# Layer 0 attention from the third batch on: scores computed once with queries on partitions, the softmax weights turned by VectorE and transfers

## The chip, the core and the metric

The kernel runs on one NeuronCore of a Trainium2 chip. TensorE (PE) multiplies matrices into PSUM banks; VectorE (DVE) reduces, copies and transposes 32x32 blocks; ScalarE (ACT) evaluates exp and other functions; GpSimd (POOL) does a few elementwise jobs; SyncE (SP) issues nearly all transfers (DMA), one after the other. Every engine works off its own instructions in order and waits on semaphores of the others. The metric is the device time of one execution in microseconds (us).

## The reference, cut to what matters

Two layers run over x (8 batches, 256 tokens, 256 features) with a context of the same shape. Each layer adds a gated cross-attention and a gated feed-forward part to x. The change touches the attention of layer 0:

```
q = Q @ Wq + bq          # Q = layernorm(x), K = V = context
k = K @ Wk + bk          # 16 heads of 16 features
v = V @ Wv + bv
scores = einsum('bhqd,bhkd->bhqk', q, k) / sqrt(16)
attn = softmax(scores, axis=-1)
out = einsum('bhqk,bhkd->bhqd', attn, v)
return out @ Wo + bo
```

Layer 0's feed-forward part ("slots") follows for the same batch, then layer 1's attention (8 heads of 128, 512 keys: 256 of the context and 256 of x), then layer 1's quantized feed-forward part over all batches.

## The kernel before, in words

Layer 1's attention is the main loop: `attention1` goes through 64 steps, one for each batch and head. A step computes scores for the two halves of the queries (line 1170), their negative maxima (VectorE, line 1171), exp (ScalarE, line 1172) and the division by the sums (lines 1173, 1174); `move_e` turns the weights with two VectorE transposes of 32x32 blocks (line 1184) and four SP transfers (line 1190) from the tile z into eT, where keys lie on partitions; `sums` multiplies them with the values (line 1226) one step later. Projections for the next heads are lines 1087 (queries), 1124 (keys), 1147 (values) and 1239 (output).

Layer 0 is ahead of it. Batches 0 and 1 run in a head stage before the loop; batches 2 to 7 are cut into pieces with costs and put into a queue (`side`), together with the slots' pieces. Each step of the loop spends a share of that queue, so that batch b's layer 0 is finished when the loop needs it: `until` forces it at head 5 of the batch before. The order that comes out is fixed when the program is built.

In layer 0 heads go in groups of four (`HG`), four groups a batch. float32 numbers are split into a rounded part hi and a rest lo, so that one matmul with single-pass operands sums hi*hi, hi*lo, lo*hi and lo*lo over 64 rows. Before the change a group of a batch past the second does this:

- `stack`: six transfers fetch the operand rows of four heads from DRAM (lines 624 and 628), where `split` had written hi and lo (line 528).
- `scores`: eight matmuls of 65 rows (line 648) with queries on partitions, four maxima (line 651), and their split into hi and lo (lines 654, 655).
- `maxima`: a TensorE transpose (line 661) and two ScalarE copies (line 664) put the maxima into further operand rows.
- `exps`: eight matmuls of 73 rows (line 674), which compute the scores a second time with keys on partitions and the maxima subtracted, and four exp of 512 columns (line 677).
- `sums`: eight matmuls of 32 columns (line 685), in float32, which the profile counts as two each; `divide`: a transpose and two small operations on VectorE (lines 708 to 711).

float32 matmuls of layer 1 count twice in the profile as well: the eight instructions of line 1226 in one step are four matmuls in the code.

Of the kernel before, what the change touches and what calls it, by code (L numbers as in the profile page):

```python
# [25 lines left out]
HG = 4  # L26
NG = H0 // HG
NROW = 4 * DK0

# [20 lines left out]
IDLE_KEY = 10  # L50
IDLE_LATENTS = 8
# [55 lines left out]
def flamingo_kernel(ctx: ExitStack, tc: tile.TileContext, a: dict, out: bass.AP):  # L107
# [62 lines left out]
    wk_n, wq_n = xs[4], cs[4]  # L170
    wk, wq = (w0.tile([P, 2, D], F32, tag=n, name=n) for n in ("wk", "wq"))
    bk_n, bq_n = (pp_.tile([P, 2], F32, tag=n, name=n) for n in ("bkn", "bqn"))
    bk, bq = (w0.tile([P, 2], F32, tag=n, name=n) for n in ("bk", "bq"))
    nc.sync.dma_start(out=cs[0], in_=c_in[0])
    nc.sync.dma_start(out=wk_n, in_=a["L0_xattn_Wk"].rearrange("(c p) n -> p c n", p=P))
    nc.sync.dma_start(out=xs[0], in_=x_in[0])
    nc.sync.dma_start(out=wq_n, in_=a["L0_xattn_Wq"].rearrange("(c p) n -> p c n", p=P))
    for t, name in ((bk_n, "L0_xattn_bk"), (bq_n, "L0_xattn_bq")):
        nc.sync.dma_start(out=t, in_=a[name].rearrange("(c p) -> p c", p=P))
# [14 lines left out]
    def load_by_place():  # L194
        for m in range(2):
            for t, name in ((bk, "L0_xattn_bk"), (bq, "L0_xattn_bq")):
                bias = a[name].rearrange("(h e) -> e h", e=DK0)
                nc.sync.dma_start(out=t[:, m : m + 1], in_=bias[m * 8 : (m + 1) * 8, :])

    def by_place():  # L200
        for t, n in ((wk, wk_n), (wq, wq_n)):
            A.copy(t.rearrange("p c (e h) -> p c e h", e=DK0), n.rearrange("p c (h e) -> p c e h", e=DK0))
        G.tensor_scalar(bq4, bq, DK0**-0.5, None, ALU.mult)

# [4 lines left out]
    pick = w0.tile([NMAX, HG], F32, tag="pick", name="pick")  # L209
    V.tensor_tensor(pick, ident[:NMAX, 1 : 1 + HG], ident[:NMAX, 1 + HG : 1 + 2 * HG], ALU.add)  # L210

    def operand_pairs(pool, n):

        pairs = []
        for i in range(n):
            q = pool.tile([NROW + NMAX, HG, S], F32R, tag=f"qs{i}", name=f"qs{i}")
            k = pool.tile([NROW + NMAX, HG, S], F32R, tag=f"ks{i}", name=f"ks{i}")
            V.tensor_copy(q[NROW : NROW + 1, :, :], blank[:1, :HG, None].to_broadcast([1, HG, S]))
            V.tensor_copy(k[NROW:, :, :], pick[:, :, None].to_broadcast([NMAX, HG, S]))
            pairs.append((q, k))  # L220
        return pairs

    blank = w0.tile([P, 2 * HG], F32, tag="blank", name="blank")
    V.memset(blank, 0.0)

    pairs_a, pairs_b = operand_pairs(pp_, 2), operand_pairs(w0, 2)
# [104 lines left out]
    slotsT = pp_.tile([P, 2, P], F32, tag="slotsT", name="slotsT", bufs=1)  # L331
# [29 lines left out]
    def prepare_slots():  # L361
        st = {}

        def load_slots():
# [7 lines left out]
            st["w2"] = pp_.tile([NSLOT, P], F32, tag="w2n", name="w2n")  # L372
# [92 lines left out]
    bq4_n = pp_.tile([P, 2], F32, tag="bq4n", name="bq4n")  # L465
    G.tensor_scalar(bq4_n, bq_n, DK0**-0.5, None, ALU.mult)

    def values_tile(pool):
# [6 lines left out]
        s: [pool.tile([P, SIDE + NMAX], F32R, tag=f"nm{s}{i}", name=f"nm{s}{i}") for i in range(3)]  # L475
        for s, pool in (("a", pp_), ("b", w0))
# [7 lines left out]
    class Batch0:  # L484
# [11 lines left out]
        def tmp(self, dtype=F32, name="t"):  # L496
            if self.b == 0:
                return own[name]
            return self.pool.tile([P, 2, S], dtype, tag="t", name=name, bufs=4)

        def halves(self, name):
            if self.b > 1:
                return self.tmp(F32R, "hi"), self.tmp(F32R, "lo")
            return (
                pp_.tile([P, 2, S], F32R, tag=f"{i}{name}{self.b}", name=f"{i}{name}") for i in ("hi", "lo")
            )
# [10 lines left out]
        def split(self, name, full):  # L517

            hi, lo = self.halves(name)
            V.tensor_copy(hi, full)  # L520
            eng = V if self.b < 2 else G
            eng.tensor_tensor(lo, full, hi.bitcast(F32), ALU.subtract)
            if self.b < 2:
                return hi, lo
            name += self.s
            d = dram.tile([2, D, S], F32, tag=f"d{name}", name=f"d{name}")
            for i, x in enumerate((hi, lo)):
                nc.sync.dma_start(out=d[i].rearrange("(m p) t -> p m t", p=P), in_=x.bitcast(F32))
            return d.rearrange("i (e h) t -> i e h t", e=DK0)
# [9 lines left out]
        def turn_c(self):  # L539
            self.cT = self.pool.tile([P, 2, S], F32, tag="cT", name="cT", bufs=1)  # L540
            A.copy(self.cT, self.turned(cs[self.b]))
# [21 lines left out]
        def query(self):  # L563
            w, bias = (wq_n, bq4_n) if self.b < 2 else (wq, bq4)
            pp = self.project(w, self.xnT)
            q = self.tmp(name="q")
            for m in range(2):
                A.activation(q[:, m, :], pp[:, m, :], AF.Identity, bias=bias[:, m : m + 1], scale=DK0**-0.5)
            self.dq = self.split("q", q)

        def key(self):
            w, bias = (wk_n, bk_n) if self.b < 2 else (wk, bk)
            pp = self.project(w, self.cT)
            k = self.tmp(name="k")
            for m in range(2):
                A.activation(k[:, m, :], pp[:, m, :], AF.Identity, bias=bias[:, m : m + 1])
# [39 lines left out]
        def stack(self, g):  # L616

            if self.b < 2:
                return self.spread(g)
            q, k = self.pairs[g % 2]  # L620
            at = slice(g * HG, (g + 1) * HG)
            for i in range(2):
                half = 2 * DK0 * i
                nc.sync.dma_start(
                    out=k[half : half + 2 * DK0, :, :].bitcast(F32), in_=self.dk[:, :, at, :]
                )
            for r in range(4):
                ins = nc.sync.dma_start(
                    out=q[r * DK0 : (r + 1) * DK0, :, :].bitcast(F32), in_=self.dq[r // 2][:, at, :]
                )  # L630
# [48 lines left out]

        def sums(self, g):  # L680

            po = self.bank()[:, :S]

            def product(kc, j):
                return T.matmul(  # L685
                    po[32 * j : 32 * j + 32, :],
                    self.ve[:, kc, g * HG + j, :],
                    self.e[j // 2][:, j % 2, kc, :],
# [29 lines left out]
        def turn_o(self):  # L718

            self.oT = self.tmp(name="oT")  # L720
            V.transpose(
                self.oT.rearrange("p c (i s) -> p (c i) s", s=32), self.o.rearrange("p c (i s) -> p (c i) s", s=32)
            )
# [15 lines left out]
    def layer0():  # L739
# [8 lines left out]
        def head(me, groups):  # L748
# [6 lines left out]
            ] + [piece(0.0, me, "stack", g) for g in groups]  # L755

        def maxima(me, g):
            return [piece(0.5, me, "scores", g, qc) for qc in range(2)] + [piece(0.1, me, "maxima", g)]

        for b in range(2):  # L760
            out[b] += head(bs[b], range(2)) + maxima(bs[b], 0)
        for b in range(B):
            me = bs[b]
            after = bs[b + 1] if 0 < b < B - 1 else None
            for g in range(NG):
                nxt = (me, g + 1) if g + 1 < NG else (after, 0)
                far = (me, g + 2) if g + 2 < NG else (after, g + 2 - NG)
                work = [piece(0.5, me, "exps", g, 0)]
                if nxt[0]:
                    work.append(piece(0.5, nxt[0], "scores", nxt[1], 0))  # L770
                work.append(piece(0.5, me, "exps", g, 1))
                if nxt[0]:
                    work.append(piece(0.5, nxt[0], "scores", nxt[1], 1))
                if g == 0:
                    work.append(piece(1.8, me, "value"))
                if after:
                    if g == 0:
                        work.append(piece(0.0, after, "norm"))
                    if g == 1:
                        work.append(piece(0.5, after, "turn_x"))  # L780
                        work.append(piece(0.5, after, "turn_c"))
                        work.append(piece(1.8, after, "query"))
                    if g == 2:
                        work.append(piece(1.8, after, "key"))
                if nxt[0]:
                    work.append(piece(0.1, nxt[0], "maxima", nxt[1]))
                work.append(piece(1.8, me, "sums", g))
                if far[0]:
                    work.append(piece(0.0, far[0], "stack", far[1]))
                work.append(piece(0.0, me, "divide", g))  # L790
                out[b] += work
        for b in range(B):
            out[b] += [piece(0.0, bs[b], "turn_o"), piece(1.8, bs[b], "finish")]
# [194 lines left out]
    for b in range(2, B):  # L988
        side.add(merge(work0[b], waiting, 1, 2))
# [12 lines left out]
    load_by_place()  # L1002
# [12 lines left out]
    for n, go in enumerate(first):  # L1015
# [3 lines left out]
        if n >= LAG:  # L1019
            second.pop(0)()  # L1020
    by_place()
# [5 lines left out]
    prep_cm.__exit__(None, None, None)  # L1027

# [15 lines left out]
    class Batch1:  # L1044
# [5 lines left out]
        def media(self):  # L1050
# [5 lines left out]
            else:  # L1056
                self.cn = at1.tile([P, 2, D], F32, tag="tn", name="cn")
            ln_apply(self.cn, cs[self.b], *ln_stats(cs[self.b], "c"))

        def latents(self):  # L1060

            b = self.b
            self.ln = at1.tile([P, 2, D], F32, tag="tn", name="ln")
# [72 lines left out]
        def value(self, hp, half, early=False):  # L1136

            if hp not in self.v:
                v = at1.tile([P, 4, 2 * P], F32, tag="v1", name="v1")
                self.v[hp] = [v[:, 0:2, :], v[:, 2:4, :]]  # L1140
            if half == 0 and early:
                self.v[hp][0] = (own["oT"], own["o"])[hp]
# [11 lines left out]
            (A.copy if half == 0 else V.tensor_copy)(self.v[hp][half], pv)  # L1154
# [58 lines left out]
        def sums(self, h):  # L1213
# [11 lines left out]
            for kc in range(4):  # L1225
                T.matmul(  # L1226
                    pi,
                    self.v[h // 2][kc // 2][:, kc % 2, (h % 2) * P : (h % 2 + 1) * P],
# [26 lines left out]
        def norm(self):  # L1255
            b = self.b
            self.xl = at1.tile([P, 2, D], F32, tag="tn", name="xl") if b < B - 1 else ffn["xl"]
# [173 lines left out]
    def attention1():  # L1431
# [24 lines left out]
        for n, (b, h) in enumerate(steps):  # L1456
# [19 lines left out]
            elif last is not None:  # L1476
                if h == 1 and b > 0:
                    bs[b - 1].project(1)
                bs[last[0]].sums(last[1])
            if h == 2 and b > 0:  # L1480
# [15 lines left out]
            if h % 2 == 1 and nxt:  # L1496
                if nxt[0] > 0 or nxt[1] > 3:
                    bs[nxt[0]].value(nxt[1] // 2, 0)
                bs[nxt[0]].value(nxt[1] // 2, 1)
# [259 lines left out]
```

## Time and profile before

| what | us |
|---|---|
| device time, median of 3 runs (914.7 to 917.16) | 915.1 |
| the profiled execution, device time | 917.64 |
| its span in the trace | 915.7 |
| PE busy | 877.0 |
| DVE busy | 639.8 |
| ACT busy | 461.9 |
| POOL busy | 143.1 |

Busy time is the union of an engine's spans. The first loop step begins at 131.2 us (its first maximum), the 17th at 339.7, the 41st at 640.9; the last weights are used at 857. Layer 0's last pieces lie before 647 us, so the loop has a stretch that is dense with layer 0 (131.2 to 339.7), one with less of it (339.7 to 640.9) and one with none. After 857 layer 1's feed-forward part follows.

### The profile page before, as it was taken

The numbers are of one execution on the slowest core, as the hardware profiler recorded it, in microseconds if no ns is written. First come the engines' busy times: TensorE is split into PE (matmuls) and PEld (weight loads), VectorE is DVE, ScalarE is ACT, GpSimd is POOL, SyncE is SP. The second block draws the span as 40 slices with busy tenths as digits, with TensorE's granted clock in tenths as the row PEclk, the third lists the DMA queues.
The fourth block names the chain that finished last, engine by engine and source line by source line (L and its number), as shares of the span: only waits on it lengthen the run. The fifth ranks groups of instructions, "written<-read, shape, count | busy, mean of one in ns | idle before, by whom it ended". The sixth has DMA issues, their size and how long they took to land. (4 is left out here: it accounts for less than half of the span.)

```text
span 915.7 us, 12787 instructions
## 1 busy us (share of the span) xinstructions
PE 877.0 (96%) x4339; PEld 636.3 (69%) x4341; DVE 639.8 (70%) x1630; ACT 461.9 (50%) x915; POOL 143.1 (16%) x183
## 2 busy tenths in 40 slices
PE   5998999999999999999999999999989999999897
PEld 4766777887777767766777667666756776776645
DVE  9675788777587766767677665766895475455387
ACT  3676646555356542555544544554364335434394
POOL 7011130201110112111011000010510010000083
PEclk9999999999999999999999999999999999999999
DMA  6712303342341332332312322212323232222112
GB/s 165 250 10 69 114 29 90 88 120 77 108 116 47 92 92 47 84 98 73 92 37 68 104 69 71 46 47 64 107 64 70 47 69 59 58 55 60 24 35 92
DMA packets 71728, 71.12 MB, mean 78 GB/s; under 512 B 14640, under 2 KB 67184, under 8 KB 71664
## 3 DMA queue, kind: packets, MB, share of 16 engines
q1 hardware_dynamic: 70032, 69.53, 29.0%
q0 software_dynamic: 1632, 0.79, 0.5%
q8 instruction: 35, 0.57, 0.3%
q14 instruction: 29, 0.24, 0.1%
HBM read 28.08 MB, written 8.39 MB: 40 GB/s over the span
## 5 line engine op out<-in xcount | busy, mean ns | idle before, releaser
L1172 ACT ACTIVATE e<-bank_m,nm 128x512 f32<-128x512 f32 x128 | 88.0, 688 | 107.5 <-DVE nm L1171 105.3
L1171 DVE TENSOR_REDUCE nm<-bank_m 128x1 f32<-128x512 f32 x128 | 87.1, 686 | 60.1 <-PE bank_m L1170 59.1
L1226 PE MATMUL bank_m<-eT,v 128*128 128x256 f32 x496 | 121.5, 382 | 4.6 <-DMA eT<-z 4.3
L1226 PEld LDWEIGHTS bank_m<-eT,v 128*128 128x128 f32 x496 | 92.4, 190 | 35.7 <-issue 16.6
L1124 PE MATMUL bank_m<-kvT,w1kv 128*128 128x512 f32 (+1 forms) x256 | 115.9, 568 | 0.0
L1147 PE MATMUL bank_m<-w1kv,kvT 128*128 128x256 f32 x480 | 111.0, 380 | 0.0
L1170 PE MATMUL bank_m<-k,q 128*128 128x512 f32 x224 | 108.9, 598 | 0.0
L1147 PEld LDWEIGHTS bank_m<-w1kv,kvT 128*128 128x128 f32 x480 | 89.4, 190 | 12.0 <-issue 0.8
L1184 DVE STREAM_TRANSPOSE z<-e 128x512 f32<-128x512 f32 x126 | 88.6, 706 | 4.3 <-DMA eT<-z 1.8
L651 DVE TENSOR_REDUCE nf<-bank_z 128x2 f32<-128x512 f32 x112 | 74.0, 680 | 20.7 <-PE bank_z L648 20.6
L270 POOL TENSOR_TENSOR rstd<-rstd,mhalf 128x2 f32<-128x2 f32 x48 | 34.6, 722 | 298.0 <-DVE rstd L269 267.7
L677 ACT ACTIVATE e<-bank_z 128x512 f32<-128x512 f32 x112 | 63.5, 598 | 32.7 <-PE bank_z L674 31.8
L1124 PEld LDWEIGHTS bank_m<-kvT,w1kv 128*128 128x128 f32 x256 | 46.4, 190 | 43.1 <-issue 38.0
L1233 ACT ACTIVATE oT<-bank_m,bv 128x256 f32<-128x256 f32 x64 | 30.4, 474 | 81.1 <-PE bank_m L1226 81.0
L1087 PE MATMUL bank_m<-kvT,w1q 128*128 128x256 f32 x256 | 64.0, 385 | 1.3 <-DVE kvT L1077 0.9
L1174 DVE TENSOR_SCALAR e<-e,rs 128x512 f32<-128x512 f32 x128 | 63.3, 495 | 2.6
L1239 PE MATMUL bank_m<-w1o,oT 128*128 128x256 f32 x256 | 59.2, 380 | 0.6 <-DVE x L1253 0.6
L1170 PEld LDWEIGHTS bank_m<-k,q 128*128 128x128 f32 x224 | 41.0, 191 | 23.4 <-issue 17.0
L1087 PEld LDWEIGHTS bank_m<-kvT,w1q 128*128 128x128 f32 x256 | 48.1, 192 | 12.4 <-issue 3.9
L1239 PEld LDWEIGHTS bank_m<-w1o,oT 128*128 128x128 f32 x256 | 48.0, 190 | 10.2 <-issue 3.2
L674 PE MATMUL bank_z<-qs,ks 73*128 73x256 f32 x224 | 49.8, 325 | 3.2 <-DVE nf L651 2.6
L1154 DVE COPY v<-bank_m 128x512 f32<-128x512 f32 x32 | 22.0, 688 | 44.0 <-PE bank_m L1147 44.0
(386 smaller groups left out, 1482.0 us busy)
## 6 DMA issues: line engine op xcount, KB each, us to landing
eT<-z SPq DMA_DIRECT2D x252, 128.0 KB, 2.7
qs<-dqb SPq DMA_DIRECT2D x96, 64.0 KB, 2.5
ks<-dkb SPq DMA_DIRECT2D x48, 128.0 KB, 2.8
c<-in_ctx_dram SPq DMA_DIRECT2D x8, 256.0 KB, 2.9
x<-in_x_dram SPq DMA_DIRECT2D x8, 256.0 KB, 2.8
w1kv<-in_L_xattn_Wkv_dram SPq DMA_DIRECT2D x4, 512.0 KB, 6.8
out_dram<-y SPq DMA_DIRECT2D x7, 256.0 KB, 2.2
dqb<-hi SPq DMA_DIRECT2D x6, 256.0 KB, 3.0
```

The lines of the kernel that those rows point to most:

```text
L651: V.tensor_reduce(full[:, 2 * half : 2 * half + 2], ps, AX.X, ALU.max, negate=True)
L677: A.activation(e[:, i, :, :], ps, AF.Exp)
L1087: T.matmul(pq[:, i, :], w1q[:, c, h * P : (h + 1) * P], self.kvT[:, c, S:], start=c == 0, stop=c == 1,)
L1124: T.matmul(pk[:, at], w1kv[:, c, h * P : (h + 1) * P], self.kvT[:, c, at], start=c == 0, stop=c == 1,)
L1147: T.matmul(pv[:, k, :], (self.mT, self.kvT[:, :, S:])[half][:, c, k * P : (k + 1) * P], w1kv[:, c, at : at + 2 * P], start=c == 0, stop=c ...
L1170: T.matmul(ps, q, self.k[h], start=True, stop=True)
L1171: V.tensor_reduce(nm[:, at], ps, AX.X, ALU.max, negate=True)
L1172: A.activation(e[:, qc, :], ps, AF.Exp, bias=nm[:, at], accum_out=sums[:, at])
L1174: V.tensor_scalar(e[:, qc, :], e[:, qc, :], rs[:, at], None, ALU.mult)
L1184: V.transpose(z[:, :, :, qc, :].rearrange("p kq kc s -> p kc kq s"), self.e[h][:, qc, :].rearrange("p (kc kq k) -> p kc kq k", kc=4, kq=4),)
L1226: T.matmul(pi, self.v[h // 2][kc // 2][:, kc % 2, (h % 2) * P : (h % 2 + 1) * P], eT[:, kc], start=kc == 0, stop=kc == 3,)
L1239: self.projected = T.matmul(self.pp[:, qc, :], self.oT[:, h, qc * P : (qc + 1) * P], w1o[:, h, :], start=h == 0, stop=h == H1 - 1,).ins
```

## The change

For batches 2 to 7 the scores are computed once. `weigh` takes two heads (a pair s of a group): four matmuls, two maxima that ScalarE takes as the bias of exp, four exp of 256 columns, and, as layer 1 does, two VectorE transposes and four transfers that turn the weights. `scores`, `maxima` and `exps` remain for batches 0 and 1. The operand stacks hold one pair of heads and are two in number; `split` writes hi and lo interleaved, and a second copy with the two exchanged for q. `sums` reads the turned weights.

```diff
         def split(self, name, full):
...
-            name += self.s
-            d = dram.tile([2, D, S], F32, tag=f"d{name}", name=f"d{name}")
-            for i, x in enumerate((hi, lo)):
-                nc.sync.dma_start(out=d[i].rearrange("(m p) t -> p m t", p=P), in_=x.bitcast(F32))
-            return d.rearrange("i (e h) t -> i e h t", e=DK0)
+            d = dram.tile([2, 2 * D, S], F32, tag=f"d{name}", name=f"d{name}")
+            hl = hl.bitcast(F32)
+            nc.sync.dma_start(
+                out=d[0].rearrange("(m p i) t -> p m (i t)", m=2, i=2), in_=hl.rearrange("p m i t -> p m (i t)")
+            )
+            for i in range(2 if name == "q" else 0):
+                nc.sync.dma_start(
+                    out=d[1].rearrange("(m p i) t -> i p m t", m=2, i=2)[1 - i], in_=hl[:, :, i, :]
+                )
+            return d.rearrange("r (g s i n) t -> r g s n i t", s=2, i=2, n=HALF)
...
-        def stack(self, g):
...
+        def stack(self, g, s):
+
+            q, k = stacks[s]
+            for r in range(2):
+                at = slice(r * HALF, (r + 1) * HALF)
+                ins = nc.sync.dma_start(out=k[at, :, :].bitcast(F32), in_=self.dk[0, g, s])
+                ins = nc.sync.dma_start(out=q[at, :, :].bitcast(F32), in_=self.dq[r, g, s])
...
+        def weigh(self, g, s):
+            q, k = stacks[s]
+            e = at0.tile([P, 2, 2, S], F32, tag="e", name="e", bufs=2)
+            z = at0.tile([P, 8, 2, 2, 32], F32, tag="e", name="z", bufs=2)
+            for i in range(2):
+                ps = self.bank().rearrange("p (c k) -> p c k", c=2)
+                for qc in range(2):
+                    T.matmul(ps[:, qc, :], q[:, i, qc * P : (qc + 1) * P], k[:, i, :], start=True, stop=True)
+                nm = small.tile([P, 2], F32, tag="nm0", name="nm0")
+                V.tensor_reduce(nm, ps, AX.X, ALU.max, negate=True)
+                for qc in range(2):
+                    A.activation(e[:, i, qc, :], ps[:, qc, :], AF.Exp, bias=nm[:, qc : qc + 1])
+                V.transpose(
+                    z[:, :, i, :, :].rearrange("p kb c s -> p c kb s"),
+                    e[:, i].rearrange("p c (kb k) -> p c kb k", k=32),
+                )
+            eT = self.e[g, s] = at0b.tile([P, 4, 2, 2, 64], F32, tag="eT0", name="eT0", bufs=3)
+            for i in range(4):
+                nc.sync.dma_start(
+                    out=eT[:, i].rearrange("p kc h x -> p (kc h x)"),
+                    in_=z[32 * i : 32 * i + 32].rearrange("p kb h c s -> p (kb h c s)"),
+                )
```

The tags e and z share two buffers, so each has one. Further edits go with it:

- The pieces of a group are now: weigh pair 0 of the next group, stack pair 0 of the one after it, sums, weigh pair 1, stack pair 1, divide. The first group of batch 2 is stacked and weighed in the queue, no longer in the head stage. A batch's values and key projection and the finish of the batch before have new places in the list, and the slots' pieces come after every second piece and no longer after every one.
- The weights wk, wq and their biases are loaded straight into their tiles in the reference's order; the copies that permuted them (`by_place`) and four small loads (`load_by_place`) go.
- The key's ScalarE copy reads its columns in a permuted order, and the output's transposes (`turn_o`) are two of 256 columns instead of one of 512 (6 batches).
- To make room: the pool of batch temporaries (tag t) has two buffers for four, layer 1's `cn`, `ln` and `xl` share one buffer (tag tn) for two, and layer 1's values are kept by halves, three in number; the second half is computed in the step that uses it first instead of the step before:

```diff
+            if h % 2 == 0 and n > 0:
+                me.value(h // 2, 1)
...
-                bs[nxt[0]].value(nxt[1] // 2, 1)
```

## The prediction

> **What bounds the kernel now.** I read the busy rows first, then the busy time in five stretches cut at loop steps, then the costliest groups, then who waits for whom.
>
> ```profile
> PE 877.0 (96%) x4339; PEld 636.3 (69%) x4341; DVE 639.8 (70%) x1630; ACT 461.9 (50%) x915; POOL 143.1 (16%) x183
> ...
> PEclk9999999999999999999999999999999999999999
> ```
> ```profile
> core 0: us, PE busy (x) PEld busy (x) DVE busy (x) ACT busy (x) POOL busy (x), PEclk, DMA share, GB/s
> 0.00:131.20 131.20, 113.04 (x707) 88.02 (x708) 98.39 (x285) 76.31 (x137) 35.71 (x60) 0.97 0.39 111
> 131.20:339.70 208.50, 204.65 (x1088) 155.13 (x1087) 154.87 (x423) 112.52 (x225) 25.87 (x32) 0.99 0.33 89
> 339.70:640.90 301.20, 297.81 (x1441) 213.20 (x1441) 209.24 (x550) 145.44 (x293) 32.10 (x43) 1.00 0.27 70
> 640.90:857.00 216.10, 210.81 (x826) 149.30 (x825) 135.71 (x303) 93.47 (x209) 19.43 (x22) 0.99 0.27 65
> ```
>
> I call the stretches head, A (dense with layer 0), B (thinner) and C (no layer 0). In A and B PE idles 3.9 of 208.5 and 3.4 of 301.2 us; DVE idles 53.6 and 92.0. So PE sets both, and PE work taken out there shortens them until DVE, the next, is full. The groups give the prices:
>
> ```profile
> L651 DVE TENSOR_REDUCE nf<-bank_z 128x2 f32<-128x512 f32 x112 | 74.0, 680 | 20.7 <-PE bank_z L648 20.6
> ...
> L648 PE MATMUL bank_z<-ks,qs 65*128 65x256 f32 x224 | 50.0, 332 | 1.0 <-ACT e L677 0.5 <-ACT qs L614 0.3
> L674 PE MATMUL bank_z<-qs,ks 73*128 73x256 f32 x224 | 49.8, 325 | 3.2 <-DVE nf L651 2.6 <-ACT qs L664 0.6
> ...
> L654 DVE CAST nmb<-nf 128x4 fp32r<-128x4 f32 x56 | 9.5, 170 | 0.4
> ...
> L655 DVE TENSOR_TENSOR nmb<-nf,nmb 128x4 fp32r<-128x4 f32 x56 | 8.8, 156 | 0.5
> ...
> L661 PE MATMUL bank_z<-ident,nmb 128*73 128x128 f32 x28 | 7.9, 282 | 1.5 <-DVE nmb L655 1.5
> ```
> ```profile
> L1184 DVE STREAM_TRANSPOSE z<-e 128x512 f32<-128x512 f32 x126 | 88.6, 706 | 4.3 <-DMA eT<-z 1.8
> ...
> L1190 SPq DMA_DIRECT2D eT<-z x252: 542/598/1699, 135.5 to 848.5; - x126
> DMA to landing us min/median/max: 2.5/2.7/4.2
> ...
>   DMA eT<-z: 1.8, 3
> ```
>
> Matmuls overlap, so one costs its share of the busy time, 50.0/224 = 0.22 us, not its own 0.33. The last fence is the path that layer 0's weights will take: a transpose of 0.70, four issues of 0.60 on SP, 2.7 to land; and VectorE already waits for its z to be read, 1.8 us in three cases (last line, from the view of line 1184).
>
> **PE.** A group loses eight matmuls and a transpose; 24 groups: 192 x 0.22 + 24 x 0.28 = 42.2 + 6.7 = 49. By the instruction orders of the two built programs, cut at the same steps: single-pass score matmuls go from 152 to 136 in the head, 174 to 100 in A, 186 to 84 in B, line 661's transposes from 9, 11 and 12 to 8, 0 and 0; A gains one group's sums and B loses one (eight at 30.0/448 x 2 = 0.13, 1.1 us). So head -3.8, A -16.3 - 3.1 + 1.1 = -18.3, B -22.4 - 3.4 - 1.1 = -26.9. PE then needs 186.4 in A and 270.9 in B.
>
> [...] The rows decide: the large matmul groups have no idle time before them, and eight of line 1226 take 1.89 us in the timeline, 0.24 each, without a gap.
>
> **DVE.** Added: 96 transposes at 0.703 (88.6/126): 2 us in the head (3), 35.9 in A (51), 29.5 in B (42). Removed: 96 small operations at 0.163 (18.3/112): 1.3, 6.8, 7.5. Maxima stay at 96, but by place -4, +7, -3 at 0.66: -2.6, +4.6, -2. One group's divide (0.44 + 0.20 + 0.33 = 1.0) moves from B to A. Net: head -2, A +34.7, B +19: DVE needs 189.6 in A and 228 in B. A is thus no longer PE's: the two are level at 186 and 190 in 208.5. B stays PE's, with DVE at 84%.
>
> **ACT.** 192 exp of 256 columns replace 96 of 512 (63.5/112 = 0.57) and 48 copies at 0.58 (32.2/56). No exp of 256 columns is in the trace; below 0.57 by half the columns, 0.28, above by the 128x256 activation with a bias (line 568), 0.47; I take 0.44, nearest the latter in form. 192 x 0.44 = 84 against 54.7 + 27.8 = 82.5: nothing (-29 to +8), covered by ACT's half-idle time.
>
> **New waits.** Two, both on transfers.
> (1) z has one buffer, so weigh's first transpose waits until the previous weigh's four transfers have landed: 3 issues x 0.60 + 2.7 = 4.5 us after its last transpose if SP is free. Line 1190's four (2.5 us) or four stack loads (1.8) ahead of them make it 6 to 7. I added up the row durations of the VectorE work that the built order puts between consecutive weighs: of 47 gaps, 10 are below 4.7 us, 26 below 6, 34 below 7, 37 below 8. The shortfalls sum to 4.9 us in A and 3.3 in B at 4.7, 18.5 and 13.2 at 6, 35.8 and 26.1 at 7, 56 and 41 at 8. Behind the waiting transpose stand layer 1's maxima, exp and, through full banks, PE. I take 5.4 us: 10 in A, in B 8, which DVE's idle time covers.
> (2) sums waits for eT on PE, with layer 1's matmuls behind it. The chain is one maximum 0.69, two exp 0.9, a transpose 0.7, four issues and landing 4.5: 6.8 bare; layer 1's like chain takes 9 to 12 from its first maximum in the trace, so 10.5. PE work from a weigh to its sums, same addition: 6.0 us at the shortest, then 7.2, 9.0, 9.4, nine more between 10.2 and 11.7, the rest longer. Shortfall: 5.6 in A (inside DVE's bound), 5 in B; at 6.8 under 1 in all, at 12 about 13 each.
> In addition the transpose waits for ACT: after the second maximum (0.68) ACT still has about 0.4 us to do, 25 weighs in A: 10 us there.
>
> **SP.** 192 more eT issues at 0.60, 48 more stack loads at 0.42 (its 144 have that median): 135 us. In A some 13 groups x (4.8 + 3.4) + 16 x 2.5 = 147 of 208: not full, but in order, which feeds (1).
>
> [...]
>
> **Edits at nothing.** The permuted key copy (line 1233's permuted 256 columns take 474 ns, line 1096's plain 471). Two transposes of 0.44 for one of 0.71, six times: 1 us. `by_place` and its loads go from the head: -1.2 of ACT, hidden behind PE. Values' second half and the shared buffers of tn and t: work moved within a step; if layer norms then wait for the turn before, at most a PE turn of 0.6 us, 21 times, in all 13, with DVE's idle time as cover in B and C and none in A.
>
> **The sum.** Head -3. A: 190 + 10 (slot) + 10 (ACT) + 4 (what PE still holds back) = 214, +5 (200 to 225). B: 271 + 3 (idle as now) + 5 (sums) + 7 (score banks that an 84% DVE frees late; 0 to 17) = 286, -15 (275 to 296). C and the end 0. Together -13: 917.6 (the profiled execution) becomes 904.6. That execution is 2.5 above the median, so **902**, with 889 to 913 as this case's own range.
>
> **Rivals.**
> - *PE's whole saving is kept* (DVE's waits fall into idle time): A 195, B 274, head -4: -44 and 871. For it: PE waits for DVE almost nowhere today. Against it: A's level engines.
> - *The z slot sets the pace* (slower): SP's in-order queue makes it 8 us from last transpose to landing. Then A is 190 + 56 = 246 less some overlap with ACT's 10, say 242 (+33), B 230 + 41 = 271 on DVE, level with PE, 290 (-11); with head -3, +19: 934. It turns slower from about 7 us on, where A (+18) cancels B and the head. For it: SP is held up to 13 us at a time for z today. Against it: those are waits for work that isn't ready, not for SP.
> - *Late weights at sums* eat B's gain: a chain of 13 us costs B about 20, so that B stays at 301 and the sum is +2: 917. The trace's chains of 9 to 12 speak against it.
> That the change doesn't do what it says is excluded by the built order: 192 score matmuls are gone.
>
> **Chances.** Forecast 0.52, full saving 0.10, slot 0.27, late weights 0.11. About 0.3% (2.7 us) is what can be told from no change. Faster is forecast and full saving, 0.62; the late weights give 0.07 of no change and 0.04 of slower, the slot 0.02 and 0.25: same 0.09, slower 0.29. The range 878 to 926 leaves out half the full saving and half of the slot case.
>
> **What would show it.** PE busy near 828, DVE near 692; A at or above 208 us with DVE over 90% of it; B at 280 to 290; idle before the weigh transposes by `eT<-z` transfers of some 10 to 25 us in all; PE idle before sums of a few us. I am wrong if A shortens by over 8 us, if the slot waits pass 50, or if SP's issues near 0.9 us each.

## The result and the profile after

The changed kernel takes 919.03 us (median of 14 runs, 914.57 to 925.08) against 915.0 (14 runs, 913.05 to 917.16): ratio 1.0045, 95% interval 1.0023 to 1.0067. It is slower by about 4 us, where 902 was forecast. Its profiled execution took 917.81 us, with a span of 916.0 (before: 917.64 and 915.7). First the busy rows and the granted clock:

```profile
PE 855.2 (93%) x4125; PEld 615.1 (67%) x4125; DVE 679.0 (74%) x1641; ACT 451.4 (49%) x961; POOL 141.9 (15%) x182
...
PEclk9989999999999979999999999999999999999999
```

The trace counts 214 fewer matmuls on PE (the change takes out 216: 192 score matmuls and 24 transposes), but PE's busy time falls by only 21.8 us (877.0 to 855.2; 828 was forecast), and it idles 60.8 us where it idled 38.7. VectorE's busy time rises by 39, not 52. ScalarE's falls by 10. Cut at the same three loop steps as in the prediction, the head, A and B are:

```profile
0.00:131.20 131.20, 110.25 (x685) 85.78 (x686) 93.72 (x270) 74.33 (x138) 34.69 (x57) 0.96 0.40 113
131.20:341.70 210.50, 191.74 (x993) 143.78 (x992) 177.37 (x444) 107.76 (x247) 26.93 (x33) 0.97 0.61 158
341.70:642.10 300.40, 291.97 (x1339) 206.79 (x1339) 227.86 (x562) 142.13 (x316) 32.51 (x44) 1.00 0.46 113
```

So A is longer by 2.0 us and B shorter by 0.8. But this cut misleads: the change moves part of layer 1's work within its steps, and A now holds 16 value matmuls (line 1201) fewer, B eight more. A fair cut goes by layer 1's progress: at the first matmul of its 1st, 17th and 35th sums (line 1226, now 1280). Before, and then after (columns: stretch, length, then PE, PEld, DVE, ACT and POOL busy with their counts, granted clock, DMA share, GB/s):

```profile
0.00:140.40 140.40, 121.43 (x757) 94.22 (x758) 105.67 (x307) 84.56 (x153) 36.32 (x60) 0.98 0.38 107
140.40:359.40 219.00, 215.96 (x1125) 162.72 (x1125) 161.01 (x438) 111.23 (x225) 27.46 (x34) 0.99 0.34 90
359.40:588.40 229.00, 225.69 (x1134) 162.10 (x1133) 160.08 (x420) 113.58 (x231) 23.47 (x30) 1.00 0.28 72
```
```profile
0.00:143.50 143.50, 120.46 (x748) 94.05 (x748) 104.85 (x301) 83.52 (x157) 36.09 (x59) 0.96 0.41 114
143.50:373.20 229.70, 212.19 (x1052) 157.10 (x1053) 185.54 (x464) 108.81 (x252) 29.35 (x37) 0.97 0.59 151
373.20:590.70 217.50, 211.59 (x1012) 150.15 (x1011) 172.75 (x414) 107.24 (x246) 21.41 (x28) 1.00 0.52 131
```

The dense stretch is 10.7 us longer and the next 11.5 shorter; the head costs 3.1, the rest gives back 2.0. In the dense stretch PE idles 17.5 of 229.7 us (3.0 of 219.0 before), while VectorE, at 81%, is not full either. So no engine's work alone sets the stretch now; PE's waits have grown, and its granted clock is 0.97 where it was 0.99. From the groups and from the waits:

```profile
L688 DVE STREAM_TRANSPOSE z<-e 128x512 f32<-128x512 f32 x96 | 63.8, 690 | 20.2 <-DMA eT<-z 17.7 <-ACT e L687 0.9 <-issue 0.6
L685 DVE TENSOR_REDUCE nm<-bank_z 128x2 f32<-128x512 f32 x96 | 62.5, 676 | 9.1 <-PE bank_z L683 8.9
...
L687 ACT ACTIVATE e<-bank_z,nm 128x256 f32<-128x256 f32 x192 | 77.3, 476 | 38.9 <-DVE nm L685 37.3
```
```profile
PE bank_z L706 <- DMA eT<-z: 12.5, 10, 2.7
```

Line 688 is weigh's transpose: VectorE stood 17.7 us before it until the one z had been carried away. Line 706 is the sums: PE stood 12.5 us there for turned weights. Both waits were named in the prediction.

### The profile page after: what moved, and what is told of

It reads as the page before. It is cut to its first block, busy times and chain, and to the rows that moved or that the text cites. A ratio compares the mean times of both kernels' runs of the same rounds, so it can differ in the third digit from the quotient of the medians.

```text
span 916.0 us, 12900 instructions
## 1 busy us (share of the span) xinstructions
PE 855.2 (93%) x4125; PEld 615.1 (67%) x4125; DVE 679.0 (74%) x1641; ACT 451.4 (49%) x961; POOL 141.9 (15%) x182
## 4 chain that ended last, share of the span: by engine, by line
PE 58%; DVE 13%; DMA 5%; SPq 4%; ACT 4%; issue 2%; POOL 1%; DVEq 0%; ACTq 0%; POOLq 0%
PE bank_m L1280 9%; PE bank_m L1201 8%; PE bank_m L1178 8%; PE bank_m L1224 8%; PE bank_m L1141 5%; PE bank_m L1293 5%; DMA eT<-z 4%; SPq L694 2%; PE bank_z L706 2%; DVE z L1238 1%; PE bank_z L550 1%; PE bank_z L683 1%; DVE z L688 1%; SPq L1244 1%; PE big L1758 1%
## 5 line engine op out<-in xcount | busy, mean ns | idle before, releaser
L1201 PE MATMUL bank_m<-w1kv,kvT 128*128 128x256 f32 x480 | 114.6, 379 | 0.2 <-ACT e L1226 0.2
L687 ACT ACTIVATE e<-bank_z,nm 128x256 f32<-128x256 f32 x192 | 77.3, 476 | 38.9 <-DVE nm L685 37.3
L1238 DVE STREAM_TRANSPOSE z<-e 128x512 f32<-128x512 f32 x126 | 87.7, 703 | 4.9 <-DMA eT<-z 2.7
L688 DVE STREAM_TRANSPOSE z<-e 128x512 f32<-128x512 f32 x96 | 63.8, 690 | 20.2 <-DMA eT<-z 17.7
L1150 ACT ACTIVATE q<-bank_m,bq 128x256 f32<-128x256 f32 x64 | 26.9, 471 | 89.8 <-PE bank_m L1141 89.8
L685 DVE TENSOR_REDUCE nm<-bank_z 128x2 f32<-128x512 f32 x96 | 62.5, 676 | 9.1 <-PE bank_z L683 8.9
```

Of the source, the lines that this page charges most:

```text
L685: V.tensor_reduce(nm, ps, AX.X, ALU.max, negate=True)
L687: A.activation(e[:, i, qc, :], ps[:, qc, :], AF.Exp, bias=nm[:, qc : qc + 1])
L688: V.transpose(z[:, :, i, :, :].rearrange("p kb c s -> p c kb s"), e[:, i].rearrange("p c (kb k) -> p c kb k", k=32),)
L1201: T.matmul(pv[:, k, :], (self.mT, self.kvT[:, :, S:])[half][:, c, k * P : (k + 1) * P], w1kv[:, c, at : at + 2 * P], start=c == 0, stop=c ...
L1238: V.transpose(z[:, :, :, qc, :].rearrange("p kq kc s -> p kc kq s"), self.e[h][:, qc, :].rearrange("p (kc kq k) -> p kc kq k", kc=4, kq=4),)
```

## The experiments

Times are medians with the kernel before measured on the same chip (914.9 to 915.6). An edit also changes the order in which the instructions are built: laid side by side, the traces differ in the order of VectorE's instructions in a quarter to a third of the places, between the kernel before and its doubled version as between the changed kernel and those without turning, without transfers and with a second z. What that alone is worth is not shown; one change of order further down was worth 6 to 7 us. The differences below are therefore those of whole builds. Four theories run through the experiments. *Price*: a removed matmul was worth its share of the busy time, 0.22 us. *Step*: it was worth only the step to the next matmul's start. *Slot* and *Transfers*: z's one buffer, or the transfers as a whole, took the gain.

**What a score matmul is worth.** The kernel before, with the maxima's matmuls issued twice:

```diff
-                for i in range(2):
+                for n in range(4 if self.b > 1 else 2):
+                    i = n % 2
                     j = 2 * half + i
```

> The kernel before with each of the 192 score matmuls of the maxima (third batch on) issued twice: as many as the change takes away, added instead, with nothing else. Theory Price (0.22 each): 915 + 42 = 957. Theory Step (0.15 each): 915 + 29 = 944; at the 0.12 of the shortest steps 938.

Measured 938.17 us (ratio 1.0255, 1.0225 to 1.0285): +23.3 us for 192 matmuls, 0.121 each. Its busy row and its group of these matmuls:

```profile
PE 900.1 (96%) x4533; PEld 660.5 (71%) x4533; DVE 643.4 (69%) x1630; ACT 462.9 (49%) x915; POOL 142.9 (15%) x183
```
```profile
L649 PE MATMUL bank_z<-ks,qs 65*128 65x256 f32 x416 | 72.7, 310 | 2.0 <-DVE x L738 1.3 <-ACT qs L614 0.3 <-ACT e L678 0.2
```

192 more instructions put the group from 50.0 to 72.7 us of busy time, 0.118 each. The lowest of the three values that were expected stands. The trace of before had said so, in its timeline:

```profile
118.42 0.72 PE L674 MATMUL bank_z<-qs,ks 73*128 73x256 f32 x4
```

Four of them take 0.72 us with one's own 0.33 in it: three steps of 0.13. From start to start, the median step of line 648 in that trace is 0.12. The group's 0.22 holds the pipeline's tail once for every two or four matmuls, and the next group's matmuls run under that tail: where a matmul of another line follows those of line 648, it starts before the last has ended in 78 of 82 places, by 0.16 us on the median.

**The change without the turning.** In weigh the transposes and the transfers are left out:

```diff
-            e = at0.tile([P, 2, 2, S], F32, tag="e", name="e", bufs=2)
-            z = at0.tile([P, 8, 2, 2, 32], F32, tag="e", name="z", bufs=2)
+            e = at0b.tile([P, 2, 2, S], F32, tag="eT0", name="eT0", bufs=3)
...
-                V.transpose(...)
...
-                nc.sync.dma_start(out=eT[:, i]..., in_=z[32 * i : 32 * i + 32]...)
+            self.e[g, s] = e.rearrange(...)
```

> Leaves out the turning of layer 0's weights from the third batch on: no transposes, no eT transfers; the sums read the unturned weights. The PE work of the changed kernel stays. Theory Price (a removed score matmul is worth the 0.22 us of its share of the busy time, and the turning eats the saving): PE's whole saving shows, 915 - 44 to 49 = 866 to 871. Theory Step (a score matmul holds PE only for the step to the next start, about 0.15 us in the trace of before, so that the saving was never over some 33): 880 to 888. Both expect a granted clock near that of before, 0.99.

Measured 889.99 us (ratio 0.9735, 0.9701 to 0.9769): the change without its price is worth 25 us, near Step and well short of Price.

```profile
PE 849.0 (95%) x4125; PEld 613.4 (69%) x4125; DVE 629.6 (71%) x1545; ACT 451.8 (51%) x961; POOL 140.5 (16%) x182
```

PE's busy time falls by 28.0 us: 192 x 0.118 = 22.7, which would leave 0.22 for each of the 24 transposes of line 661 (a remainder, not measured by itself).

**The transposes without the transfers.**

```diff
-            z = at0.tile([P, 8, 2, 2, 32], F32, tag="e", name="z", bufs=2)
+            z = at0b.tile([P, 8, 2, 2, 32], F32, tag="eT0", name="eT0", bufs=3)
...
-                nc.sync.dma_start(out=eT[:, i]..., in_=z[32 * i : 32 * i + 32]...)
+            self.e[g, s] = z.rearrange(...)
```

> Leaves out the eT transfers of layer 0 from the third batch on: the weights are transposed in blocks by VectorE as in the changed kernel, and the sums read the blocks where they lie. Theory Transfers (slots of z, SP's queue, landings before the sums and the traffic cost what was hoped for): within 5 us of the kernel without any turning. Theory VectorE (its 67 us of transposes make the stretch dense with layer 0 its own): 908 to 919, close to the changed kernel.

Measured 900.58 us (ratio 0.9845, 0.981 to 0.9879): by these builds the transposes cost 10.6 us, the transfers the other 18.5. Neither theory had it alone.

```profile
PE 851.2 (95%) x4125; PEld 612.6 (68%) x4125; DVE 677.1 (75%) x1641; ACT 451.0 (50%) x961; POOL 141.7 (16%) x182
```

VectorE's busy time rises by 47.5 us for 96 transposes, 0.49 each, though one lasts 0.69: it, too, overlaps its neighbours (in the trace of the changed kernel the transpose at 438.32 us lasts 0.69, and VectorE's next instruction begins 0.62 after it).

**A second buffer for z.** It needs no space: e, z and the split pair hl go round in one tag.

```diff
-                hl = at0.tile([P, 2, 2, S], F32R, tag="hl", name="hl", bufs=1)
+                hl = at0.tile([P, 2, 2, S], F32R, tag="e", name="hl", bufs=3)
...
-            e = at0.tile([P, 2, 2, S], F32, tag="e", name="e", bufs=2)
-            z = at0.tile([P, 8, 2, 2, 32], F32, tag="e", name="z", bufs=2)
+            e = at0.tile([P, 2, 2, S], F32, tag="e", name="e", bufs=3)
+            z = at0.tile([P, 8, 2, 2, 32], F32, tag="e", name="z", bufs=3)
```

> The changed kernel with e, z and the split pair hl in one rotation of three buffers, in the same space, so that z no longer waits for the transfers of the z before it. Theory Slot (17.7 us of VectorE's waits before the weigh transposes set the pace of the dense stretch): 905 to 911. Theory Step or Late sums: the wait is in VectorE's slack, 917 to 921. If the z slot wait only moves to e, ACT waits instead and the time stays at 919.

Measured 906.64 us (ratio 0.9912, 0.9882 to 0.9943): this build is 12.4 us faster than the changed kernel, of the transfers' 18.5, and now faster than the kernel before. Run again:

> The kernel with the rotation of three buffers once more, on the same chip as the next two, as their base and for a narrower interval: 904 to 909, 0.7 to 1.2 per cent below the kernel before. At 913 or more the second buffer's gain was chance.

Measured 905.54 us (ratio 0.9896, 0.9881 to 0.991). What VectorE waited for before line 688, in this kernel:

```profile
  DMA eT<-z: 2.6, 3
```

17.7 us have become 2.6. Little of the wait moved to e: the transfers of line 694 are also what these wait for (who, us, times):

```profile
  POOL hl L513: 29.4, 2
  PE bank_z L706: 6.2, 6
  DVE z L688: 2.6, 3
  ACT e L687: 1.1, 2
```

ScalarE stands 1.1 us before its exponentials; GpSimd, which has idle time, stands before the split pair hl. The dense stretch and the next, by layer 1's progress, in the kernel without turning, the one without transfers, and this one:

```profile
145.90:354.00 208.10, 205.41 (x1052) 154.32 (x1053) 158.58 (x407) 108.61 (x250) 29.21 (x37) 0.99 0.37 102
354.00:565.10 211.10, 210.56 (x1011) 149.61 (x1011) 151.06 (x372) 107.17 (x246) 20.76 (x27) 1.00 0.32 84
```
```profile
143.20:361.50 218.30, 209.86 (x1052) 156.02 (x1053) 185.06 (x464) 108.68 (x252) 28.89 (x37) 0.98 0.36 98
361.50:572.70 211.20, 210.52 (x1012) 149.51 (x1012) 170.70 (x414) 107.03 (x246) 21.41 (x28) 1.00 0.32 83
```
```profile
139.10:361.10 222.00, 209.37 (x1057) 156.21 (x1056) 186.84 (x469) 111.23 (x258) 30.38 (x39) 0.98 0.61 156
361.10:577.80 216.70, 212.70 (x1012) 150.95 (x1011) 172.43 (x414) 107.25 (x246) 21.24 (x28) 0.99 0.52 131
```

The transposes cost 10.2 us where layer 0 is dense (3.4 of them are more lost clock, 5.1 against 1.7, see the last section) and nothing (0.1) in the next stretch, where VectorE has 40 us of idle time left to take them. The transfers with one slot then cost 11.4 and 6.3 us, with two 3.7 and 5.5. Of what remains, the largest part that the view of PE's waits names is the wait for landings before the sums, 6.2 us.

**Other queues for the eT transfers.** `nc.gpsimd` or `nc.scalar` in place of `nc.sync`, on the kernel with the rotation and, for POOL, on the changed kernel as it is.

> The kernel with the rotation of three buffers (906.6 us), and its eT transfers of layer 0 issued on POOL's queue in place of SP's. Theory Order (the 6 us that the transfers still cost there come from the queue's order on SP: weights stand behind stack loads and layer 1's transfers, and those behind them): 901 to 903. Theory Landing (what is left is the 2.5 us of four issues and 2.7 of landing ahead of the sums): 905 to 908. If POOL, held by the waits for the transposes, makes the layer norms late: 910 or more.

> The changed kernel, z with its one slot, and the eT transfers of layer 0 issued on POOL's queue in place of SP's. Theory Order: the slot is held by SP's queue, so that it comes free by 1 to 2 us earlier and most of the 12 us that the second buffer brought come back: 908 to 912. Theory One slot (four issues and a landing, 5.2 us, are enough to hold VectorE): 916 to 920.

> The kernel with the rotation of three buffers, and its eT transfers of layer 0 issued on ACT's queue in place of SP's. Theory Order: 901 to 904. If ACT, which then stands at each weigh for VectorE's second transpose with the exponentials of layer 1 behind it, becomes the late one: 910 or more.

Measured 925.53 (ratio 1.0094, 1.006 to 1.0129), 949.52 (1.0374, 1.0348 to 1.0399) and 935.76 us (1.0232, 1.0197 to 1.0267). All three are slower than the same kernel on SP, by 19 to 20, 30 and 29 to 30 us; theory Order falls. On POOL the median from issue to landing is 3.3 us in place of 2.7 (3.1 with one z). What makes these builds slower isn't separated further. The pair on POOL is a second dose of the slot, though: with one z VectorE waits 44.1 us (28 times) for it, with two 4.0, and the time differs by 24. Here the wait of the kernel with one z on POOL:

```profile
DVE z L688 <- DMA eT<-z: 44.1, 28, 5.2
```

**One transpose for two** per weigh, of 128x1024, with the rotation:

```diff
-                V.transpose(z[:, :, i, :, :]..., e[:, i]...)
+            V.transpose(
+                z.rearrange("p kb i c s -> p (i c) kb s"), e.rearrange("p i c (kb k) -> p (i c) kb k", k=32)
+            )
```

> The kernel with the rotation of three buffers (906.6 us), its two transposes of 128x512 per weigh made one of 128x1024: 48 fewer instructions on VectorE, but the one waits for all four exponentials. Theory VectorE (the transposes' own time is what is left of the turning's cost): 903 to 906. Theory Late sums (the landing ahead of the sums is): the chain gets longer by some 0.5 us, 907 to 911.

Measured 908.18 us (ratio 0.9935, 0.9914 to 0.9956), 1.5 to 2.6 above the same kernel with two. No gain is seen; that the later start outweighs the saved instructions is not shown.

**The pieces' places.** The text on the change says that the slots' pieces used to come after every piece; that is a slip. Both kernels put one after every second piece, and the change starts one place later, (2, 2) for (1, 2). Set back to (1, 2), and moved on to (3, 2):

> The kernel with the rotation of three buffers, and the spacing of the slots' pieces among layer 0's set back from (2, 2) to the (1, 2) of the kernel before. If the order of the pieces costs what the transfers leave: 901 to 904. If not: 905 to 908.

> The kernel with the rotation of three buffers, and the slots' pieces of the first batches one place later among layer 0's, (3, 2) in place of (2, 2). If the place of these long chains in the dense stretch sets part of what is left: 4 us or more to either side of 906.6. If it was chance that (1, 2) cost 6 us: 905 to 908.

Measured 912.72 (ratio 0.9966, 0.9948 to 0.9985) and 903.6 us (0.9879, 0.9857 to 0.9902). (1, 2) costs 6 to 7 us; (3, 2) has the lowest median of the kernels that do all the work, though only 2 us below (2, 2), with overlapping intervals.

**Layer 0 spread thinner**, with the rotation and, as a control, in the kernel before:

```diff
-        due = {ready[b]: 6 * b - 2 for b in range(1, B)}
+        due = {ready[b]: 7 * b - 3 for b in range(1, B)}
```

> The kernel with the rotation of three buffers, and layer 0 spread thinner over the loop: due steps of 7b - 3 in place of 6b - 2. Theory Dense (VectorE and the transfers hold PE only where layer 0 is dense; with more of layer 1's work between two weighs the waits fall into slack): 893 to 902, near the kernel without eT transfers (900.6) or below. If PE's total and the head set the time: 905 to 909.

> The kernel before with the due steps of 7b - 3 and nothing else: a control. PE has gaps of only 6 us in its loop there, so every theory expects no change beyond 3 us: 912 to 918.

Measured 923.51 (ratio 1.0089, 1.0063 to 1.0115) and 930.32 us (1.0171, 1.0145 to 1.0198): both expectations missed, the control too. The edit puts the last batches' chains late: in the control PE stands for a result of the slots at 700 us and behind VectorE's work on the feed-forward's weights (wg_s) at 716, and by layer 1's progress the control is 5.5 us ahead of the kernel before at 676 us of the latter's time and 13.5 behind at 710, where it stays.

```profile
700.49 1.44 PE L959 MATMUL bank_s<-svo,alT 128*128 128x256 f32 x4 [1.96 <-DVE x L961]
...
715.81 1.19 PE L1087 MATMUL bank_m<-kvT,w1q 128*128 128x256 f32 x2 [3.37 <-DVE wg_s L1305]
```

The kernel with the rotation and this edit is 3 us slower than its base over the dense stretch, level with it at 650 us and 20 behind from 700 us on. So the theory got no support, and what is lost at the end hides what thinning might be worth by itself.

**An idle place filled.** Where score matmuls of the maxima and of the exponentials stood at the loop's start, PE now waits 3.44 us for a layer norm, and the clock falls after it, to 0.50 for 3.41 us. Before, where the layer norm's transposes follow matmuls of lines 648, 674 and 583 without a wait, and after:

```profile
123.17 0.60 PE L287 MATMUL bank_m<-ident,ln 128*128 128x128 f32 x4
```
```profile
122.28 1.23 PE L277 MATMUL bank_m<-ident,ln 128*128 128x128 f32 x4 [3.44 <-DVE ln L265]
```

```diff
         first.latents()
+        fill_in, w = bank("m"), ident.bitcast(BF16)
+        for _ in range(28):
+            T.matmul(fill_in[:, :S], w[:, :P], w, start=True, stop=True)
         first.turn("l")
```

> The kernel with the rotation of three buffers, and 28 matmuls on the identity (their sums are not used) where PE stands idle for 3.4 us at the loop's start, a place that the removed score matmuls used to fill. Theory Clock (an idle stretch of a few us is followed by 1.7 to 5.1 us lost at half the granted clock, so that gaps cost more than themselves): no loss of clock near 122 us and 903 to 905. If the loss of clock has nothing to do with the gap: no change, or up to 2 us more.

Measured 910.59 us (ratio 0.995, 0.9935 to 0.9964), 5 above its base. The clock stayed at 1.00 there (0.63 and 0.51 in the base between 120 and 124 us), but the build put weigh's first matmuls behind the filling, and in the profiles it is 3.5 us behind its base by layer 1's first sums and 8.4 by the eleventh. The clock's part of the time is thus not settled by it.

## Why the prediction was wrong

Forecast and measurement side by side, in us. "Saving" is the change without the turning against before: forecast, the prediction's rival of the full saving; measured, the run without the turning. "Turning" is what comes on top. The measured rows are those of the profiled executions, cut by layer 1's progress, which the prediction's cut only approximates.

| | saving, forecast | measured | turning, forecast | measured |
|---|---|---|---|---|
| head | -4 | +5.5 | +1 | -2.4 |
| A, dense | -13.5 | -10.9 | +18.5 | +21.6 |
| B, next | -27 | -17.9 | +12 | +6.4 |
| rest | 0 | -2.6 | 0 | +0.6 |
| medians of the whole | -44 | -25 | +31 | +29 |

- **The step that failed** is the first price: "one costs its share of the busy time, 50.0/224 = 0.22 us", and with it PE's 49 us. Doubling gave 0.118 to 0.121 each and removal 28.0 in all. The full saving is worth 25 us, not 44. That 19 is the miss: 902 + 19 = 921 against 919. The nearer price stood in the trace of before: the bf16 matmuls of 256 columns of line 512 step at 0.109 us on the median; the score matmuls, at 0.12, lie a tenth above.
- **That the totals agree so well is partly luck.** At the measured prices the forecast's 44 us of saving become 28, which is 16 of the 19. By stage, in these profiles, the head accounts for 9.5 of the miss, and the price for only 1.7 of that: the kernel without turning waits there 3.4 us for a layer norm and loses 3.4 us more to the clock than the kernel before. A, B and the rest together gained 5 to 6 us more than the price gives.
- **The turning's cost** was right in sum, 31 against 29, but not term by term. VectorE's own bound of 190 in A was not reached (177 by the same cut): a transpose was priced at its own 0.70, and it adds 0.49. The 10 us in A for a transpose that waits for ScalarE came out as 0.9, once:

```profile
DVE z L688 <- ACT e L687: 0.9, 1, 0.9
```

- **Wait (1), the slot.** The wait was sized well: 18 us forecast (10 in A and 8 in B), 17.7 measured (8.3 and 5.4 by the prediction's cut, 4.1 just ahead of A); the landing came 5.4 us after weigh's last transpose on the mean, as taken. The rival's 8 us was reached only as the maximum. The price to the kernel, 10 in A and nothing in B, came out as 12.4 to 13.5. The median from issue to landing on SP was 2.7 us in the changed kernel, as in the kernel before.
- **Wait (2), late weights at sums**: 10.6 forecast for A and B together, 12.5 measured; with the second z 6.2 are left.
- **Edits at nothing.** PE's waits for layer norms, priced at nothing, are 3.4 and 2.6 us in the changed kernel against 0.6 before, and the clock fell to 0.50 after both, for 3.4 and 10.2 us.
- **Rivals.** The rival of late weights named 917, close to the 919 measured, and B at 301, close to 300.4 by the prediction's cut. Its cause isn't the measured one: it charged B some 20 us of waiting for weights, and PE waits 4.2 us for them there. B missed its 286 mostly because PE's saving there was put too high: at 0.118 and 0.22 PE needs 282 in B, not 271. A neither kept the full saving nor grew by 33, as the other two rivals had it.
- **Stated tests.** A at or above 208 and 10 to 25 us of idle time before the weigh transposes: held. B at 280 to 290, PE near 828, VectorE near 692 and over 90% in A: failed (300.4, 855, 679, 84%), all from prices per instruction. SP's issues kept their 0.60. None of the three signs of being wrong appeared, though the forecast failed: none of them tested the price of a matmul.
- **The head** was to gain 3 and lost 3.1 in this execution. The removed matmuls there had stood in a place where PE now waits (3.44 us). But the head of the kernel with the rotation took 142.2 and 139.1 us in two profiles, so that 3 us are within the scatter.
- **The exponentials** of 256 columns took 0.476, just above the bound of 0.47; ScalarE, busy for 49% of the span, had room for it.

With a matmul at 0.118 the gain before the price of turning (25 us) is below that price (29), and the answer is "no gain". The change is mended by its buffers: with the rotation it beats the kernel before by 1.04% (0.9 to 1.19), with (3, 2) by 1.21% (0.98 to 1.43).

## What to carry to other kernels

Price a short instruction by what one more of it adds, the step from start to start in a run of equals, and not by a group's busy time over its count (here 0.118 to 0.121 us and not 0.22): the tail of a pipeline belongs to the group once, not to each member. Where two costs of opposite sign nearly cancel, the sign hangs on such prices, so price both with the same ruler and test the larger one by doubling it. A buffer that is freed by a transfer can be worth a second one where its writer works in order and has other work behind the wait: here most of 17.7 us of waiting went with it, and 12.4 to 13.5 us of the kernel; look for tiles of equal size that can go round together before giving up for want of space.

## Hardware that was not expected

In the profiles of before and after the granted clock falls to 0.50 in spells, most of them during or soon after a gap in PE's work, and the gap shown here cost more than itself. In the changed kernel's profile PE stood 2.62 us before 333.1 us; then:

```profile
332.00:334.00 2.00, 0.89 (x4) 0.81 (x5) 1.78 (x7) 0.84 (x2) 1.47 (x3) 1.00 0.85 198
334.00:336.00 2.00, 2.00 (x8) 1.57 (x6) 1.61 (x5) 0.84 (x2) 0.66 (x2) 0.55 0.88 210
336.00:338.00 2.00, 1.98 (x8) 1.20 (x7) 1.36 (x3) 0.00 (x0) 0.39 (x1) 0.50 0.68 182
```
```profile
329.76 0.74 PE L683 MATMUL bank_z<-kt,qt 65*128 65x256 f32 x4
...
335.33 1.54 PE L683 MATMUL bank_z<-kt,qt 65*128 65x256 f32 x4
```

The same four matmuls take 0.74 us before and 1.54 after. The clock is the last column but two; it stays at 0.50 for 10.24 us. Added up over windows of 2 us, the lost clock is worth 6.8 us in the profile of before and 11.9 in that of after, in single losses of 1.7, 3.4 or 5.1 (without a last spell at the trace's end). A loss came with gaps of 3.4 and 2.1 us (before 122.3 and 143.5 us, after), but also of 1.7 (before 54.0 us, in before), and in before one from 326.9 us on followed none above 0.63, while one of 2.7 in after (before 198.9 us) had none. In the clock records of these two traces every half-clock spell is 3.41, 6.83 or 10.24 us long (but for the last of each, cut off by the end of the trace), and the distances from the start of one spell to the start of the next are whole multiples of 3.41 (the shortest 20.5 us, the longest 580.3). Why is not shown. Around the gap of 2.7, which had no spell, PE was busy for 2.01 and 1.57 us of the 3.4 us on the two sides of 197.6:

```profile
194.20:197.60 3.40, 2.01 (x10) 1.42 (x8) 3.40 (x10) 2.37 (x6) 1.45 (x2) 1.00 0.61 139
197.60:201.00 3.40, 1.57 (x18) 0.98 (x19) 2.40 (x9) 0.91 (x3) 0.24 (x1) 1.00 0.65 176
```

In the profile of before, PE was busy for 44% of the 3.4 us from 849.1 us on, with a gap of 1.9 in them, and a half-clock spell followed; but one also followed 3.4 us in which PE was busy for 79% (from 323.5 us). So neither the gap's length nor PE's busy share tells, in these two traces, where a spell follows.

The clock also fits the scatter: spans of the changed kernel run from 912.8 us at a mean clock of 0.994 to 923.3 at 0.978. At 0.994, the one clock among them that the kernel before also reached, that kernel spans 912.3 to 913.8 us in five executions, so that at equal clock no difference is seen, on one execution of the changed kernel. Most of the spells came with gaps of PE, though: how much of the 4 us between the kernels is clock and how much the gaps themselves, no run here separates.
